# Smaller stated times for VectorE's eigenvector operations, a second weight's sums moved, and fewer operations behind the last broadcast product

## The chip, the cores and the metric

The kernel runs on one core of one Trainium2 chip. The metric is the device time of one execution in microseconds (us), given as the median of several runs. Engines are named as in the profile: PE (TensorE's matmuls), PEld (its weight loads), DVE (VectorE), ACT (ScalarE), POOL (GpSimd) and SP (SyncE, which issues most of the DMAs).

## The reference, cut to what matters

A batch of 128 graphs of 64 nodes with 256 features (8192 rows) goes through four layers, each `x = layernorm(x + layer(x))`. Layer 0 is three graph convolutions. Layer 1 goes through the eigenvectors `U` of a Laplacian of the one 64x64 matrix `adj`. Layer 2 (LSTMs over windows) and layer 3 (attention) follow.

```python
# layer 0: aggregate with adj*S (S is adj here), three weights
weighting = adj * S
h = relu(einsum('nm,bmh->bnh', weighting, x @ W1))
h = relu(einsum('nm,bmh->bnh', weighting, h @ W2))
out = einsum('nm,bmh->bnh', weighting, h @ W3)
# layer 1
deg = sum(A, axis=0) + sum(A, axis=1) - diagonal(A)
L_norm = d_inv_sqrt[:, None] * (diag(deg) - A) * d_inv_sqrt[None, :]
_, U = eigh(L_norm)
h = relu(einsum('mn,bnd->bmd', U.T, features) @ W1 + b1)
out = einsum('nm,bmd->bnd', U, h @ W2 + b2)
```

`eigh` is therefore needed once, on a 64x64 matrix, before layer 1 can begin. It doesn't depend on layer 0.

## The kernel before, in words

**Layer 0 and the eigenvectors run together.** The function `layer0` walks over 16 groups of 512 rows. For a group, `burst` mixes rows with the squared adjacency (64x64 blocks), `weigh` applies the first weight, `seven` computes the second and (except in the last two groups, which use `plain`) the third weight's product by a Strassen scheme of seven block products, and `mix_rows` mixes the result and adds it to the rows. All of these put matmuls on PE; DVE makes the sums of blocks and adds PE's results (`VL`), ACT copies and applies relu. `sums_of_weights` makes four sums of blocks of a weight on DVE, once for the second weight and once for the third.

**The eigenvector pass** is the generator `eigen`. It tridiagonalizes the matrix in 62 steps of 24 DVE instructions, one matmul (`mm(pq, L, AQ)`) and two ACT operations each, bisects for the eigenvalues in six passes, runs a chain of 63 pairs (`t`, named `tw` in the profile, then `D2`, named `D`), and finds the eigenvectors. Nearly all is on DVE, in operations on 64x1 to 128x64 elements. At its end it broadcasts two columns over a matrix with `rows` (the eigenvalues `lam`, then the product `co_[7]`), decides signs (`co_[9]` to `co_[12]`), multiplies (`pu`), and spreads `U` and its transpose into the two 128x128 block matrices `u2` and `ut2`, which layer 1 needs.

**How the two are put in order.** The order of instructions on PE, DVE and ACT is the order in which Python emits them (`manual_schedule`). Python keeps a clock `now`, which each layer-0 matmul advances by a stated time. After each matmul `between()` resumes `eigen` if the time it asked for has come. `eigen` knows its own time by `free[0]`: the class `Timed` passes each DVE operation on and adds a stated time, `least` plus 0.0009 us for each element over 64. `soon()` asks to be resumed 0.45 us before `free`, `full()` at `free`; `until` is the stated time at which a result of PE or ACT is there. So `least` doesn't change what DVE computes: it sets how far apart `eigen`'s instructions are put in the queues, and after which of layer 0's matmuls its own matmuls stand on PE. When layer 0 has been emitted, `while eig:` emits what is left of `eigen`.

```python
self.free[0] = max(self.free[0], self.until[0]) + self.least + 0.0009 * max(0, np.prod(out.shape[1:]) - 64)
```

Before, `least` is 0.25 us at first and for `VL`; 0.285 in the bisection, 0.22 in the chain of pairs, and 0.25 after it.

**After layer 0**, `phase_a.close()` gives back its buffers, the LSTM weights are loaded by SP, and a planner (`Plan`, with its own stated costs) orders layers 1 to 3; all of its instructions carry the helper line L162. Its first matmuls are those of layer 1, `ps<-u,X`. In the profile, DVE operations of `layer0` and `eigen` carry L52, layer 0's matmuls L966 (`burst`: L1031), the eigenvector pass's matmuls L312 (`mm`) and the transposes L323, L644 and L739; ACT's square roots in the steps are L397, its copies behind `burst` L1037.

Of the kernel before, what the change touches and what calls it, by code (L numbers as in the profile page):

```python
# [13 lines left out]
ALU = mybir.AluOpType  # L14
AX = mybir.AxisListType

N = 64
# [24 lines left out]
class Timed:  # L42
# [1 line left out]


    def __init__(self, engine, free, until):
        self.engine, self.free, self.until, self.least = engine, free, until, 0.25

    def __getattr__(self, name):
        def give(out, *args, **kw):  # L50
# [224 lines left out]
def eigen(tc, stack, a, ident, cst, u2, ut2, now, free):  # L275
# [10 lines left out]
    until = [0.0]  # L286
    V, S, PE = Timed(nc.vector, free, until), nc.scalar, nc.tensor
# [5 lines left out]
    def sb(shape, tag):  # L293
        uid[0] += 1
        return wp.tile(shape, F32, tag=tag, name=f"{tag}_{uid[0]}")

    def ps(shape, tag):
        uid[0] += 1
        return pp.tile(shape, F32, tag=tag, name=f"{tag}_{uid[0]}")

    W = 2 * N
    C = {n: cst[:N, i, :] for i, n in enumerate(CONSTS)}
    C["eye"] = ident[:N, :N]

    def soon():
        return max(free[0], until[0]) - 0.45

    def full(turns=0):
        return max(free[0], until[0]) + 0.6 * turns

    def mm(out, lhsT, rhs):
        PE.matmul(out, lhsT, rhs, start=True, stop=True)  # L312
        now[0] += 0.2
        until[0] = now[0] + 0.5
# [46 lines left out]
    eye = C["eye"]  # L361
# [20 lines left out]
    for i in range(N - 2):  # L382
# [9 lines left out]
                               op1=ALU.mult, accum_out=rest)  # L392
# [6 lines left out]
        for update in late[1:]:  # L399
# [11 lines left out]
                               op1=ALU.mult, accum_out=v)  # L411
# [11 lines left out]
                               op1=ALU.mult, accum_out=av)  # L423
# [4 lines left out]
                               op1=ALU.mult, accum_out=c2)  # L428
# [47 lines left out]
    def rows(col, n, tag):  # L476
        b = sb([N, N], "bc")
        V.tensor_scalar(b, C["ones"], col, None, op0=ALU.mult)
        yield full()
        p = ps([N, n, N], tag)  # L480
        mm(p, b, cst[:N, 0:n, :])
        return p

    co = cp.tile([N, 20], F32, name="co")
    co_ = [co[:, j:j + 1] for j in range(20)]
    nrm, s1, s1s, s2e, hs = co_[1:6]
# [11 lines left out]
    t0, t1, t2, big, ae, sg = w_[11:17]  # L498
# [6 lines left out]
    lo, h, top, tgt, at, to = co_[14:20]  # L505
# [51 lines left out]
    idx = cst[:, CONSTS.index("idx"), 1:FAN + 1]  # L557
    Q = cp.tile([W, HALF, FAN], F32, name="Q")
    M = cp.tile([W, FAN, HALF], F32, name="M")
    V.least = 0.285  # L560
    yield soon()
    for _ in range(PASSES):
        V.tensor_scalar(h2, h2, 1.0 / (FAN + 1), None, op0=ALU.mult)
# [5 lines left out]
        for k in range(1, HALF):  # L569
# [10 lines left out]
                               op0=ALU.is_lt, op1=ALU.mult)  # L580
# [18 lines left out]
    V.tensor_scalar(dl, d2, lam2, None, op0=ALU.subtract)  # L599
    D2 = cp.tile([W, N], F32, name="D2")  # L600
    V.tensor_copy(D2[:, N - 1:], dl[:, 0:1])
    V.least = 0.22
    for k in range(1, N):
        c = N - 1 - k
        t = sb([W, 1], "tw")
        V.reciprocal(t, D2[:, c + 1:c + 2])
        V.tensor_scalar(D2[:, c:c + 1], t, es2[:, k:k + 1], dl[:, k:k + 1], op0=ALU.mult, op1=ALU.add)
        yield soon()
    V.least = 0.25
    D = cp.tile([N, 2, N], F32, name="D")  # L610
    for k in range(2):
        V.tensor_scalar(D[:, k, :], D2[k * N:(k + 1) * N, :], 1e15, -1e15, op0=ALU.min, op1=ALU.max)
# [35 lines left out]
    rn = co_[13]  # L648
# [55 lines left out]
    V.tensor_mul(co_[7], co_[7], co_[6])  # L704
    pl = (yield from rows(lam, 1, "pa"))[:, 0, :]
    V.tensor_scalar(t0, pl, lam, 1e-12, op0=ALU.subtract, op1=ALU.add)
    V.reciprocal(t0, t0)
    V.tensor_mul(t0, t0, C["off"])
    V.tensor_copy(t1, pl)
    V.tensor_mul(t1, t1, t1)  # L710
    V.tensor_reduce(co_[8], t1, AX.X, ALU.max)
    V.tensor_scalar(co_[8], co_[8], nrm, (8.0 * 2.0 ** -24) ** 2, op0=ALU.mult, op1=ALU.mult)
    pp_ = (yield from rows(co_[7], 1, "pa"))[:, 0, :]
    rowdot(hs, pp_, t0)
    V.tensor_scalar(hs, hs, -1.0, 1.0, op0=ALU.mult, op1=ALU.add)
    V.tensor_mul(hs, hs, hs)
    V.tensor_mul(hs, hs, co_[8])
    yield soon()
    V.tensor_scalar(co_[9], s1, s1, 2.0, op0=ALU.mult, op1=ALU.mult)
    V.tensor_tensor(co_[9], co_[9], hs, ALU.is_gt)  # L720
    V.tensor_scalar(co_[10], s2e, s2e, 2.0, op0=ALU.mult, op1=ALU.mult)
    V.tensor_tensor(co_[10], co_[10], co_[8], ALU.is_gt)
    yield soon()
    V.tensor_scalar(co_[11], s2e, 0.0, -2.0, op0=ALU.is_gt, op1=ALU.mult)
    V.tensor_scalar(co_[11], co_[11], co_[10], 1.0, op0=ALU.mult, op1=ALU.add)
    V.tensor_scalar(co_[12], s1, 0.0, -2.0, op0=ALU.is_gt, op1=ALU.mult)
    V.tensor_scalar(co_[12], co_[12], 1.0, co_[11], op0=ALU.add, op1=ALU.subtract)
    V.tensor_scalar(co_[12], co_[12], co_[9], co_[11], op0=ALU.mult, op1=ALU.add)
    V.tensor_mul(co_[12], co_[12], rn)


    yield full()
# [1 line left out]
    mm(pu, Z, QT)  # L734
    UT = cp.tile([N, N], F32, name="UT")
    V.tensor_scalar(UT, pu, co_[12], None, op0=ALU.mult)
    yield full()
    pt = ps([N, N], "pa")
    PE.transpose(pt, UT, C["eye"])  # L739
    until[0] = now[0] + 0.7  # L740
    U = cp.tile([N, N], F32, name="U")
    V.tensor_copy(U, pt)
    V.memset(u2, 0.0)
    V.memset(ut2, 0.0)
    yield full()
    for out, lhsT in ((u2, UT), (ut2, U)):
        p2 = ps([2 * N, N], "pa")
        for h in range(2):
            mm(p2[h * N:(h + 1) * N, :], lhsT, C["eye"])
        for h in range(2):  # L750
            V.tensor_copy(out[h * N:(h + 1) * N, h * N:(h + 1) * N], p2[h * N:(h + 1) * N, :])


ROWS = 8192
# [76 lines left out]
def kernel(  # L831
# [26 lines left out]
    V, S, PE = nc.vector, nc.scalar, nc.tensor  # L858
# [5 lines left out]
    def tl(pool, shape, tag, **kw):  # L864
        uid[0] += 1
        return pool.tile(shape, F32, tag=tag, name=f"{tag}_{uid[0]}", **kw)
# [7 lines left out]
    pa = phase_a.enter_context(tc.tile_pool(name="pa", bufs=1))  # L874
# [54 lines left out]
    u2 = keep.tile([P, P], F32, name="u2")  # L929
    ut2 = keep.tile([P, P], F32, name="ut2")  # L930
# [34 lines left out]
    def mm(out, lhsT, rhs, start=True, stop=True, **kw):  # L965
        PE.matmul(out, lhsT, rhs, start=start, stop=stop, **kw)  # L966
        now[0] += 2 * max(0.00084 * rhs.free_size(), 0.112)
        between()
# [8 lines left out]
    def quads(c):  # L977
        for m in (slice(0, N), slice(N, P)):
            for h, hs in enumerate((slice(0, N), slice(N, P))):
# [3 lines left out]
    B11, B12, B21, B22 = (aw2[:, r:r + 2, c:c + 512] for r in (0, 2) for c in (0, 512))  # L983
# [14 lines left out]
    second = ((None, B11, B21, B22, tw[:, 2], B12, tw[:, 1], tw[:, 0]),  # L998
              (None, A11, A12, ss[:, 2], A22, ss[:, 0], ss[:, 1], A21))
    third = ((None, D11, D21, D22, tv[:, 2], tv[:, 3], tv[:, 1], tv[:, 0]),  # L1000
             (None, H11, H12, H12, H22, sh[:, 0], sh[:, 1], H21))
    free = [0.0]
    VL = Timed(V, free, now)
    spare = [lambda: tl(pa, [P, D], "spare")]
    pending = []

    def step(then=None):

        while pending:
            pending.pop(0)()  # L1010
        if then:
            pending.append(then)
        if norms:
            norms.pop(0)()
# [4 lines left out]
    def sums_of_weights(w, b12):  # L1019
        VL.tensor_sub(w[7], w[3], b12)  # L1020
        VL.tensor_sub(w[5], b12, w[1])
        VL.tensor_sub(w[6], w[3], w[5])
        VL.tensor_sub(w[4], w[2], w[6])

# [33 lines left out]
    def seven(n, product, c11, c12, c21, c22, last):  # L1058
# [4 lines left out]
        def add(dst, b):  # L1063
            VL.tensor_add(dst, dst, b)
            if last is relu:
                relu(dst, dst)
# [36 lines left out]
    def weigh(t):  # L1103
        p = bank()
        run(p, [(m1[:, k, t * P:(t + 1) * P], aw1[:, k, :]) for k in range(2)])
        step(lambda: relu(h1[:, t, :], p))

    def mix_rows(g, t):
# [3 lines left out]
        def result():  # L1112
            x2 = rows_of(order[g])[:, t:t + 2, :]
            VL.tensor_add(x2, p, x2)
            norms.extend(scalar_norm(tc, small, x2, half, spare))
# [12 lines left out]
    def layer0():  # L1128
        n = NT // 4
        burst(m1, rows_of(order[0]), 0)  # L1130
        step()
        for t in range(4):
            weigh(t)
        step()
        sums_of_weights(second[0], B12)
        for c in (0, 2):
            burst(m2, h1, c)
        step()
        for g in range(n):
            sums_second()  # L1140
            for j in range(2):
                q = [h2[:, 4 * c + 2 * j:4 * c + 2 * j + 2, r:r + 256] for r in (0, 256) for c in (0, 1)]
                for _ in seven(256, by_second(j), *q, relu):
                    pass
                if j == 0 and g + 1 < n:
                    burst(m1, rows_of(order[g + 1]), 0)
                if j == g == 0:
                    sums_of_weights(third[0], D12)
            q = [s3[:, r:r + 2, c:c + P] for r in (0, 2) for c in (0, P)]
            w3 = seven(P, by_third, *q, S.copy) if g < n - PLAIN else plain()  # L1150
            next(w3)
            next(w3)
            if g < n - PLAIN:
                VL.tensor_add(sh[:, 0], H21, H22)
                VL.tensor_sub(sh[:, 1], sh[:, 0], H11)
            for t in range(4):
                if g + 1 < n:
                    weigh(t)
                if t == 0 and g < n - PLAIN:
                    VL.tensor_sub(H21, H11, H21)  # L1160
                    VL.tensor_sub(H12, H12, sh[:, 1])
            for _ in range(4):
                next(w3)
            if g + 1 < n:
                burst(m2, h1, 0)
            next(w3)
            if g + 1 < n:
                burst(m2, h1, 2)
            for t in (0, 2):
                mix_rows(g, t)  # L1170
        step()

    eig.extend([0.0, eigen(tc, phase_a, adst[:N, :], ident, eig_c, u2, ut2, now, free)])
    with tc.manual_schedule(engines={mybir.EngineType.PE, mybir.EngineType.DVE, mybir.EngineType.Activation}):
        pt = bank()
        PE.transpose(pt[:N, :P], adst, ident)
        for h in range(2):
            hs = slice(h * N, (h + 1) * N)
# [64 lines left out]
    V, S, G, Q = (Noted(plan, e) for e in ("DVE", "ACT", "POOL", "SP"))  # L1243
# [585 lines left out]
```

## Time and profile before

| what | value |
|---|---|
| median of 3 runs | 2280.58 us (2280.14 to 2281.84) |
| the profiled execution, its own time | 2277.23 us |
| its span, first to last instruction | 2275.4 us |
| mean granted TensorE clock | 0.995 |
| PE busy | 2233.0 us (98%), 20612 instructions |
| DVE busy | 1772.5 us (78%), 5868 instructions |
| ACT busy | 1189.5 us (52%), 2892 instructions |
| layer 1's first matmul (L162) | at 834.18 us |

The times of instructions below come from the one profiled execution, counted from the start of its span. Its own time is 1.83 us over its span, and 3.35 us under the median of the three timed runs. A "group" is the stretch of layer 0 from one group of 512 rows to the next, 50.5 us of PE's time in the middle of layer 0. An "x4" in a row counts instructions; a matmul of fp32 data stands there as two, so four matmuls of the program are x8.

### The profile page before, as it was taken

The page shows a single profiled execution, that of the slowest core. Times are in us where ns is not written, and L with a number is a line of the kernel's source. Part 1 is how long each engine was busy: PE and PEld are TensorE (multiplying, and loading weights), DVE is VectorE, ACT ScalarE, POOL GpSimd, SP SyncE. Part 2 cuts the span into 40 slices and gives each one's busy share as a digit, 9 for nine tenths or more (in the row PEclk, how much of TensorE's full clock was granted, in tenths as well). Part 3 has the DMA queues.
Part 4 walks back from the last instruction along what each step waited for, and adds up shares of the span by engine and source line. Part 5 has one row for each costly group of instructions (what it writes and reads, how often), then busy time and mean ns, then how long its engine had stood idle before and what let it go on. Part 6 is the DMA issues. An engine that isn't in the chain of part 4 may idle for free.

```text
span 2275.4 us, 52244 instructions
## 1 busy us (share of the span) xinstructions
PE 2233.0 (98%) x20612; PEld 1990.8 (87%) x20612; DVE 1772.5 (78%) x5868; ACT 1189.5 (52%) x2892; POOL 137.0 (6%) x315
## 2 busy tenths in 40 slices
PE   8999999999999989999999999999999999999997
PEld 6888888887788778999999999999999999999985
DVE  5888777776888879765967977977877887578977
ACT  3444444443434435665655655655656555566554
POOL 0000000000000010000100000000010010000012
PEclk9999999999999999999999999999999999999999
DMA  7000000000000031000111211211221211001331
GB/s 245 11 11 11 11 11 11 11 20 11 11 11 1 1 126 57 11 11 20 66 40 48 78 57 50 87 57 41 87 66 40 78 66 39 31 21 65 117 107 59
DMA packets 80117, 107.93 MB, mean 47 GB/s; under 512 B 23296, under 2 KB 64256, under 8 KB 79872
## 3 DMA queue, kind: packets, MB, share of 16 engines
q1 hardware_dynamic: 79520, 104.32, 14.1%
q8 instruction: 162, 2.65, 0.5%
q14 instruction: 83, 0.68, 0.1%
q10 hardware_dynamic: 352, 0.28, 0.0%
HBM read 57.64 MB, written 45.09 MB: 45 GB/s over the span
## 4 chain that ended last, share of the span: by engine, by line
PE 91%; DVE 6%; issue 1%; ACT 1%; DMA 1%; POOL 0%; SPq 0%; ACTq 0%; DVEq 0%; POOLq 0%
PE ps L162 58%; PE ch L966 14%; PE ps L966 10%; PE b L966 7%; PE ps L1031 2%; PE pa L312 1%; DVE w L162 1%; DVE D L52 1%; DVE tw L52 1%; DVE X L162 1%; DVE gates L162 0%; DVE st L162 0%; DVE v L162 0%; ACT gates L162 0%; DVE h L52 0%
## 5 line engine op out<-in xcount | busy, mean ns | idle before, releaser
L162 PE MATMUL ps<-w,wih 128*128 128x128 f32 (+2 forms) x2944 | 572.0, 298 | 0.3 <-ACT gates L162 0.3
L162 PE MATMUL ps<-w,sums 128*128 128x128 f32 (+2 forms) x3104 | 476.3, 293 | 0.1
L162 PEld LDWEIGHTS ps<-w,wih 128*128 128x128 f32 x2944 | 453.1, 191 | 26.5 <-issue 6.8
L162 PEld LDWEIGHTS ps<-w,sums 128*128 128x128 f32 x3104 | 422.7, 191 | 14.3 <-ACT gates L162 1.9
L162 ACT ACTIVATE gates<-gates,cbi 128x256 f32<-128x256 f32 (+4 forms) x736 | 314.0, 479 | 171.8 <-DVE gates L162 169.9
L162 DVE TENSOR_TENSOR gates<-gates,ps 128x512 f32<-128x512 f32 (+4 forms) x408 | 233.7, 583 | 171.1 <-PE ps L162 158.0
L162 ACT COPY gates<-ps 128x512 f32<-128x512 f32 (+4 forms) x408 | 204.2, 506 | 252.3 <-PE ps L162 245.4
L162 PE MATMUL ps<-hs,whh 128*128 128x128 f32 (+1 forms) x896 | 181.2, 284 | 0.1
L162 PE MATMUL ps<-w,whh 128*128 128x128 f32 (+1 forms) x896 | 181.2, 284 | 0.0
L162 ACT ACTIVATE gates<-ps,cbi 128x128 f32<-128x128 f32 (+2 forms) x368 | 119.5, 384 | 42.9 <-PE ps L162 42.5
L162 PEld LDWEIGHTS ps<-hs,whh 128*128 128x128 f32 x896 | 139.8, 191 | 0.3 <-DVE hs L162 0.3
L162 PEld LDWEIGHTS ps<-w,whh 128*128 128x128 f32 x896 | 139.8, 191 | 0.0
L975 ACT ACTIVATE h<-h 128x512 f32<-128x512 f32 x96 | 60.5, 630 | 150.9 <-DVE h L52 150.9
L966 PE MATMUL ch<-m,tw 128*128 128x256 f32 x512 | 124.7, 381 | 3.1 <-ACT h L1077 1.7
L966 PE MATMUL b<-ss,aw 128*128 128x256 f32 x512 | 121.9, 379 | 0.0
L966 PE MATMUL ps<-aw,m 128*128 128x512 f32 x256 | 116.0, 606 | 1.5 <-DMA aw<-in_a_w_dram 1.5
L966 PEld LDWEIGHTS ch<-m,tw 128*128 128x128 f32 x512 | 94.9, 190 | 18.6 <-DVE h L52 3.4
L966 PEld LDWEIGHTS b<-ss,aw 128*128 128x128 f32 x512 | 96.8, 190 | 12.9
L162 POOL TENSOR_SCALAR rs<-mv 128x2 f32<-128x2 f32 x96 | 23.5, 255 | 1325.1 <-DVE mv L162 1323.7
L966 PEld LDWEIGHTS ps<-aw,m 128*128 128x128 f32 x256 | 48.3, 194 | 55.7 <-issue 51.4
L1037 ACT COPY m<-ps 128x512 f32<-128x512 f32 x96 | 51.2, 587 | 75.5 <-PE ps L1031 75.0
L162 PE MATMUL ps<-hs,sums 128*128 128x128 f32 (+1 forms) x448 | 90.6, 284 | 0.0
(373 smaller groups left out, 4139.2 us busy)
## 6 DMA issues: line engine op xcount, KB each, us to landing
far<-w SPq DMA_DIRECT2D x42, 512.0 KB, 2.9
w<-far SPq DMA_DIRECT2D x168, 128.0 KB, 3.1
X<-rest SPq DMA_DIRECT2D x24, 512.0 KB, 3.3
out_dram<-X SPq DMA_DIRECT2D x64, 128.0 KB, 1.8
rest<-XA SPq DMA_DIRECT2D x12, 512.0 KB, 2.6
rest<-X SPq DMA_DIRECT2D x12, 512.0 KB, 2.8
XA<-in_x_dram SPq DMA_DIRECT2D x22, 256.0 KB, 6.9
aw<-in_a_w_dram SPq DMA_DIRECT2D x3, 1024.0 KB, 10.2
```

The lines of the kernel that those rows point to most:

```text
L52: return getattr(self.engine, name)(out, *args, **kw)
L162: getattr(e, name)(*[real(x) for x in args], **{k: real(v) for k, v in kw.items()})
L312: PE.matmul(out, lhsT, rhs, start=True, stop=True)
L966: PE.matmul(out, lhsT, rhs, start=start, stop=stop, **kw)
L975: S.activation(dst, src, AF.Relu)
L1031: PE.matmul(p[h][m, k, t, :], src[hs, t, f], sqT2[hs, hs], start=True, stop=True)
L1037: S.copy(to[:, h, c:c + 2], p[h])
```

## The change

1. **Stated times.** `least` becomes 0.21 for `eigen` from the start (0.25 before), 0.278 in the bisection (0.285), 0.21 in the chain of pairs (0.22) and after it (0.25). `VL`, layer 0's own stated times, is set back to 0.25.
2. **The second weight's sums** (`sums_of_weights(second[0], B12)`, four DVE additions of 128x1024 elements) are emitted in the first group after the second of four `weigh` calls, no longer after the fourth.
3. **The end of `eigen`.** The second broadcast (`rows(co_[7])`) is emitted right after the first; work that doesn't need its result (`co_[8]`, both halves of `co_[10]` to `co_[12]`, the factor `rn`) is emitted while it is under way; behind the product `rowdot(hs, pp_, t0)` stand four more operations where there were thirteen. `u2` is filled straight from `UT`, ahead of the transposition that gives `U`, and the two memsets move ahead of it.

```diff
-        self.engine, self.free, self.until, self.least = engine, free, until, 0.25
+        self.engine, self.free, self.until, self.least = engine, free, until, 0.21
...
-    V.least = 0.285
+    V.least = 0.278
...
-    V.least = 0.22
+    V.least = 0.21
     for k in range(1, N):
...
-    V.least = 0.25
+    V.least = 0.21
...
     V.tensor_scalar(t0, pl, lam, 1e-12, op0=ALU.subtract, op1=ALU.add)
+    V.tensor_copy(t1, pl)
+    pp_ = (yield from rows(co_[7], 1, "pa"))[:, 0, :]
+    there, until[0] = until[0], 0.0
     V.reciprocal(t0, t0)
     V.tensor_mul(t0, t0, C["off"])
-    V.tensor_copy(t1, pl)
     V.tensor_mul(t1, t1, t1)
     V.tensor_reduce(co_[8], t1, AX.X, ALU.max)
     V.tensor_scalar(co_[8], co_[8], nrm, (8.0 * 2.0 ** -24) ** 2, op0=ALU.mult, op1=ALU.mult)
-    pp_ = (yield from rows(co_[7], 1, "pa"))[:, 0, :]
+    yield soon()
+    V.tensor_scalar(co_[9], s1, s1, 2.0, op0=ALU.mult, op1=ALU.mult)
...
+    V.tensor_mul(co_[12], co_[12], rn)
+    V.tensor_mul(co_[11], co_[11], rn)
+    until[0] = max(until[0], there)
+    yield soon()
     rowdot(hs, pp_, t0)
     V.tensor_scalar(hs, hs, -1.0, 1.0, op0=ALU.mult, op1=ALU.add)
-    V.tensor_mul(hs, hs, hs)
-    V.tensor_mul(hs, hs, co_[8])
...
+    V.tensor_scalar(hs, hs, hs, co_[8], op0=ALU.mult, op1=ALU.mult)
     V.tensor_tensor(co_[9], co_[9], hs, ALU.is_gt)
...
     V.tensor_scalar(co_[12], co_[12], co_[9], co_[11], op0=ALU.mult, op1=ALU.add)
-    V.tensor_mul(co_[12], co_[12], rn)
...
     V.tensor_scalar(UT, pu, co_[12], None, op0=ALU.mult)
+    V.memset(u2, 0.0)
+    V.memset(ut2, 0.0)
     yield full()
+    spread(u2, UT)
     pt = ps([N, N], "pa")
     PE.transpose(pt, UT, C["eye"])
     until[0] = now[0] + 0.7
     U = cp.tile([N, N], F32, name="U")
     V.tensor_copy(U, pt)
-    V.memset(u2, 0.0)
-    V.memset(ut2, 0.0)
     yield full()
-    for out, lhsT in ((u2, UT), (ut2, U)):
-        p2 = ps([2 * N, N], "pa")
...
+    spread(ut2, U)
...
     VL = Timed(V, free, now)
+    VL.least = 0.25
...
         for t in range(4):
             weigh(t)
+            if t == 1:
+                sums_of_weights(second[0], B12)
         step()
-        sums_of_weights(second[0], B12)
```

`spread(out, lhsT)` is the old loop's body: two matmuls with the identity and two DVE copies. In the built programs nothing after layer 1's first matmul differs: PE, DVE, ACT, POOL and SP have the same instructions in the same order from there on.

More of the change, by code (lines that the diff above doesn't have):

```diff
@@ L712, in eigen @@
     V.tensor_scalar(co_[8], co_[8], nrm, (8.0 * 2.0 ** -24) ** 2, op0=ALU.mult, op1=ALU.mult)
-    pp_ = (yield from rows(co_[7], 1, "pa"))[:, 0, :]
+    yield soon()
+    V.tensor_scalar(co_[9], s1, s1, 2.0, op0=ALU.mult, op1=ALU.mult)
+    V.tensor_scalar(co_[10], s2e, s2e, 2.0, op0=ALU.mult, op1=ALU.mult)
+    V.tensor_tensor(co_[10], co_[10], co_[8], ALU.is_gt)
+    V.tensor_scalar(co_[11], s2e, 0.0, -2.0, op0=ALU.is_gt, op1=ALU.mult)
+    V.tensor_scalar(co_[11], co_[11], co_[10], 1.0, op0=ALU.mult, op1=ALU.add)
+    yield soon()
+    V.tensor_scalar(co_[12], s1, 0.0, -2.0, op0=ALU.is_gt, op1=ALU.mult)
+    V.tensor_scalar(co_[12], co_[12], 1.0, co_[11], op0=ALU.add, op1=ALU.subtract)
+    V.tensor_mul(co_[12], co_[12], rn)
+    V.tensor_mul(co_[11], co_[11], rn)
+    until[0] = max(until[0], there)
+    yield soon()
     rowdot(hs, pp_, t0)
     V.tensor_scalar(hs, hs, -1.0, 1.0, op0=ALU.mult, op1=ALU.add)
-    V.tensor_mul(hs, hs, hs)
-    V.tensor_mul(hs, hs, co_[8])
-    yield soon()
-    V.tensor_scalar(co_[9], s1, s1, 2.0, op0=ALU.mult, op1=ALU.mult)
+    V.tensor_scalar(hs, hs, hs, co_[8], op0=ALU.mult, op1=ALU.mult)
     V.tensor_tensor(co_[9], co_[9], hs, ALU.is_gt)
[L721 to L727, printed above, removed]
     V.tensor_scalar(co_[12], co_[12], co_[9], co_[11], op0=ALU.mult, op1=ALU.add)
-    V.tensor_mul(co_[12], co_[12], rn)
     yield full()
@@ L736, in eigen, with spread @@
     V.tensor_scalar(UT, pu, co_[12], None, op0=ALU.mult)
+    V.memset(u2, 0.0)
+    V.memset(ut2, 0.0)
     yield full()
+    def spread(out, lhsT):
+        p2 = ps([2 * N, N], "pa")
+        for h in range(2):
+            mm(p2[h * N:(h + 1) * N, :], lhsT, C["eye"])
+        for h in range(2):
+            V.tensor_copy(out[h * N:(h + 1) * N, h * N:(h + 1) * N], p2[h * N:(h + 1) * N, :])
+    spread(u2, UT)
     pt = ps([N, N], "pa")
@@ L742, in eigen @@
     V.tensor_copy(U, pt)
-    V.memset(u2, 0.0)
-    V.memset(ut2, 0.0)
     yield full()
-    for out, lhsT in ((u2, UT), (ut2, U)):
-        p2 = ps([2 * N, N], "pa")
[L748 to L751, printed above, removed]
+    spread(ut2, U)
 ROWS = 8192
```

## The prediction

> **What bounds the kernel now.** I read the page first: PE is busy for 98% of the span, and the chain that ended last is 91% PE. So time can only be won where PE stands idle or runs at a lower clock, and lost where it is made to wait. PE's timeline up to 900 us shows such places; two are touched here.
>
> The end of the eigenvector pass (PE's timeline; in brackets the idle time ahead of a row and who ended it):
>
> ```profile
> 826.36 1.98 PE L966 MATMUL ps<-s,sqT 128*128 128x512 f32 x4
> 828.18 0.38 PE L1187 MATMUL ps<-adT,ones 128*128 128x128 f32 x2
> 828.75 0.29 PE L312 MATMUL pa<-eig_c,bc 64*64 64x64 f32 x2 [0.19 <-DVE bc L52]
> 829.99 0.33 PE L312 MATMUL pa<-AQ,Z 64*64 64x64 f32 x2 [0.95 <-DVE junk L52]
> 832.72 0.24 PE L739 MATMUL pa<-ident,UT 64*64 64x64 f32 x1 [2.40 <-DVE UT L52]
> 833.27 0.33 PE L312 MATMUL pa<-ident,UT 64*64 64x64 f32 x4 [0.31 <-DVE U L52]
> 834.16 0.37 PE L312 MATMUL pa<-ident,U 64*64 64x64 f32 x2 [0.56 <-DVE u L52]
> ```
>
> Layer 0's last matmul ends at 828.56; layer 1's first starts at 834.18. Between them PE has 1.2 us of work and 4.4 us of idle time: the eigenvector pass ends late, with nothing to cover it.
>
> The start (PE's and DVE's timeline):
>
> ```profile
> 25.64 3.78 PE L966 MATMUL ch<-m,aw 128*128 128x256 f32 x8 [3.57 <-ACT m L1037]
> ...
> 46.50 1.89 PE L966 MATMUL ch<-ss,tw 128*128 128x256 f32 x8
> 48.23 1.03 PE L966 MATMUL b<-ss,aw 128*128 128x256 f32 x4
> ```
> ```profile
> 18.40 0.28 DVE L52 TENSOR_SCALAR AQ<-pa,c 64x64 f32<-64x64 f32 x1 [3.67 <-PE pa L312]
> 18.60 1.21 DVE L52 TENSOR_TENSOR tw<-aw 128x1024 f32<-128x1024 f32 x1
> ```
>
> PE stands for 3.57 us, because ACT's copies wait behind a square root (L397, 24.44), which waits for DVE, which from 18.60 to 23.52 makes the second weight's sums. The eight matmuls behind the gap take 3.78 us; eight such take 1.73 later (46.50 to 48.23, start to start). The granted clock says why (PE busy in column 2, clock after the counts):
>
> ```profile
> 21.54:24.96 3.42, 0.53 (x37) 0.39 (x28) 2.85 (x10) 0.52 (x2) 0.00 (x0) 1.00 1.10 349
> 24.96:28.37 3.41, 2.73 (x7) 2.19 (x8) 1.75 (x3) 1.59 (x4) 0.00 (x0) 0.50 1.10 349
> 28.37:31.78 3.41, 3.41 (x10) 2.69 (x9) 1.38 (x5) 0.59 (x1) 0.00 (x0) 0.50 1.07 338
> ```
>
> From 50 to 550 us PE is never idle for more than 0.15 us. The counterpart is DVE's slack, in DVE's waits from 79.6 to 231 us (three groups):
>
> ```profile
> DVE junk L52 <- PE pa L312: 10.8, 13, 1.4
> DVE XA L52 <- PE ps L966: 3.7, 4, 1.5
> DVE q L52 <- ACT q L397: 2.1, 4, 0.7
> ```
>
> With the smaller rows it is 19.0 us, 6.3 us a group: DVE gets to a point early and waits for a matmul that Python placed late.
>
> **What the skill says.** "TensorE: Matmul & The Clock Gate" (Part 1: The HAM clock gate) has PE fall to half clock after an idle window of about 3.4 us, on a free-running grid. The trace agrees on window and halves: windows with PE busy 15% (above), 17% (830.50) and 33% (2264.08) are followed by clock 0.50, ones with 48% and 53% (2182.16, 847.56) are not. The same page (Part 2) keeps matmuls in program order, and its table makes the other engines' queues strict FIFO; so a matmul put ahead of its operand stops all of PE, as the 2.40 us above. "Vector Engine (DVE) Microarchitecture Reference" (5.2 Measured stream behaviour) gives 1.04 ns a column plus about 75 ns an instruction. 512-column additions agree (0.60 us apart), but dependent one-column operations don't: the chain's pairs stand 0.507 us apart, so I price small ones by the trace.
>
> **The change, part by part.**
>
> *Stated times, tail.* The built orders have the same 78 eigenvector matmuls; before, none of layer 0's stands behind the last, after, 262 PE instructions do, which by the rows' durations is about 79 us. So `u2` is there long before layer 1. Its first matmul still needs DVE: `ps1`'s bank is free after one of the last row additions or `rs_row`, both at DVE's end; 828.56 plus 0.7 gives 829.3, not 834.2: **-4.9**. The half clock from 833.9 to 837.3 loses 3.4/2 = 1.7: it goes, **-1.7**. But ACT must now normalize the last rows (four operations, 829.24 to 831.4 before, in the shadow of the tail) beside layer 1's copies: **+1.0** (0 to 2). Sum -5.6. Behind it the streams are the same, so the shift should carry to the end. The 5 MB of LSTM weights, issued at 826.20 and busy to about 841, are first needed near 867: not late.
>
> *Sums of the second weight.* In the new order they come behind `dm` (14.26) instead of 18.60, so DVE is done at 19.2, but AQ's and LV's memsets now stand behind them, ACT's LV copy behind these, and three relus behind that copy. By durations: relus end 21.3, the bursts 22.7, the step's matmul 23.1, the square root starts 24.0, PE 25.2: **-0.4** (+1 to -1.5). But PE now works between 19 and 23, so the worst window is some 37 to 46% busy: I take it that the clock stays up: **-3.1** (half of 25.64 to 31.78; 0 if not).
>
> *Stated times, steps.* Between two groups' block sums DVE has 163 instructions before and about 192 after: 29 more are 1.2 steps. A group's DVE time without waits is 44.4 us (79.6 on); less 13.0 for layer 0's 19 operations that is 5.2 a step, near 4.8 by 433 us. So 1.2 steps add 6.3 us to a wait of 6.3: DVE is full in the first four groups, later keeps about 2 us (waits 8.3, added 5.9). The stated step, 24 x 0.21 = 5.04, is about true; at 0.25 it was 6.0. Where the slack is gone, a wait left over reaches PE; I take 0.5 us in each of four groups: **+2.0** (0 to +6).
>
> *Chain of pairs and the end.* A pair takes 0.507 and is stated as 0.42 (0.44 before): 63 pairs make DVE 5.5 us late against 4.2. Before, that cost PE 1.33 us at 793 and 0.20 at 798. After, the last busy group holds 39 pairs (19.8), 19 of layer 0's (13.0), 88 others (0.21 each, 18.7): 51.5 against 49.6 of PE, and six exchanges with PE at 0.3: 3.7; less the 1.5 of before: **+2.0** (-1.5 to +5). Bisection fits: a pair stands 0.555 apart, stated 0.556.
>
> *Fewer operations behind the product.* 2.7 us (829.7 to 832.4) shrink to about 1.0, but the end is covered by layer 0 now: **0**; were that cover gone, -1.7. Moved memsets and `spread` likewise 0. No step that moves issues a DMA, and POOL's and SP's orders stay as they were.
>
> **Sum:** -5.6 - 0.4 - 3.1 + 2.0 + 2.0 = -5.1 on the profiled 2277.23, 2272.1. That execution lies 3.35 under the median; the same shift gives **2275.5** for the median. 0.2% is 4.6 us, about what a measurement of this kernel can tell from no change.
>
> **Rivals.**
> 1. *Slower: DVE in lockstep.* With no lead left, each step's `mm` (62) meets a column copy not quite done, and PE pays the hop; 0.31 us as ahead of 833.27. 62 x 0.31 = 19.2 in place of 2.0: 2275.5 + 17.2 = **2292.7**. It turns to slower by 0.2% at 0.19 us a step. For it: DVE's slack is used up early; against it: PE's matmuls are some 4% slower than Python's clock (a group's stated times sum to 48.3, its span is 50.5), which gives DVE about 2 us a group.
> 2. *Cold start.* The window's grid falls on the gap: -5.1 + 3.1, **2278.6**. For it: 37% is near 33%, which fell.
> 3. *The tail is only traded.* Layer 1 then waits for DVE and ACT (DVE is full from 848 to 880): 2 of 5.6 come through, **2279.1**. Against: those stretches start later by the same amount.
> 4. *No move:* refuted by the orders.
>
> **How the numbers follow.** Main case 0.58 (beyond 0.2%: 0.47), cold start 0.16 (0.02), traded tail 0.13 (0), lockstep 0.13 (slower 0.11). Faster 0.49, same 0.39, slower 0.12. Low end: no new stalls (-5.1 - 2.0 - 3.5), 2270. High end: the middle of rivals 1 and 3, 2284; it leaves out about 0.15.
>
> **What would show it.** Right: layer 1's first matmul right behind L1196 (before: L1187), no half clock there; clock 1.00 from 15 us on; DVE's waits for `pa` under 2 us a group to 400 us. Wrong: PE idle `<-DVE LV` in many steps (rival 1), clock 0.50 near 25 us (2), a new gap of PE past 829 us (3).

## The result and the profile after

The changed kernel takes **2308.43 us** (median of 4 runs, 2306.11 to 2309.28), the kernel before 2280.61 us beside it; the ratio is 1.012, 95% interval 1.0102 to 1.0137. The forecast was 2275.5 us: it missed by 33 us, and on the wrong side.

The profiled execution of the changed kernel took 2307.74 us (span 2306.0). Layer 1's first matmul starts at 860.01 us where it started at 834.18, so 25.8 us are lost ahead of it. What follows takes 1445.9 us against 1441.3. The order of instructions there is the same on every engine, and 1441.3 comes from an execution that was 3.4 us under its kernel's median; one experiment below has 1441.3 too, again in an execution 3.4 us under its median, and the others lie between 1442.7 and 1445.7. I don't ascribe this part to the change.

What was foreseen at the end is there. PE's timeline of the kernel after (start, duration, instruction; in brackets the idle time ahead of it and who ended it):

```profile
857.89 1.96 PE L973 MATMUL ps<-s,sqT 128*128 128x512 f32 x4
859.69 0.38 PE L1196 MATMUL ps<-adT,ones 128*128 128x128 f32 x2
860.01 0.33 PE L162 MATMUL ps<-u,X 64*64 64x64 f32 x2
860.84 2.09 PE L162 MATMUL ps<-u,X 64*64 64x64 f32 x126 [0.51 <-DVE rs_row L1197]
```

No eigenvector matmul is left here; one wait of 0.51 us stands where 4.4 us were idle. The loss lies earlier, in a line of the page that I had not thought about. The group of layer 0's Strassen products on the sums `tw`, after (busy time, mean ns; then the idle time of PE ahead of them, and what ended it):

```profile
L973 PE MATMUL ch<-m,tw 128*128 128x256 f32 x512 | 128.1, 389 | 26.1 <-DVE h L52 14.0 <-ACT h L1085 12.0
```

The same group before:

```profile
L966 PE MATMUL ch<-m,tw 128*128 128x256 f32 x512 | 124.7, 381 | 3.1 <-ACT h L1077 1.7 <-DVE h L52 1.2
```

So PE waits for layer 0's own additions on DVE (`h`, L52) and copies on ACT (L1085). And DVE is not full: this is the table of busy time in the stretch of groups 1 to 8 (PE, PEld, DVE, ACT, POOL, then the clock), first of the kernel before, then of the kernel after.

```profile
79.60:483.40 403.80, 403.80 (x3585) 336.36 (x3584) 320.55 (x1500) 181.38 (x480) 17.55 (x48) 1.00 0.03 12
```
```profile
87.20:513.70 426.50, 411.97 (x3599) 335.17 (x3598) 356.72 (x1756) 179.43 (x493) 17.46 (x48) 1.00 0.03 11
```

DVE works 356.7 of 426.5 us, 84%; PE is idle for 14.5 us at full clock. Two engines that both have time to spare wait for each other.

The second place is at the start, on DVE (timeline of the kernel after), and what it does to PE:

```profile
39.12 1.28 DVE L52 TENSOR_TENSOR tv<-aw 128x512 f32<-128x512 f32 x2
44.98 0.16 DVE L1202 TENSOR_TENSOR dbb<-dbb,dbl 128x2 f32<-128x2 f32 x1 [4.58 <-DMA dbb<-in_d_b_dram]
45.05 1.41 DVE L52 TENSOR_TENSOR tv<-aw,tv 128x512 f32<-128x512 f32 x2
```
```profile
25.60 1.99 PE L973 MATMUL ch<-m,aw 128*128 128x256 f32 x8 [2.06 <-ACT m L1045]
...
52.68 2.07 PE L973 MATMUL ch<-m,tw 128*128 128x256 f32 x4 [5.31 <-ACT h L1085]
```

The first row is the start as I predicted it: a shorter gap, and eight matmuls at full clock (1.99 us, 3.78 before). The second is new. `dbb` is a bias of layer 3, added up by a line that stands outside the hand-ordered part. The scheduler placed it in DVE's queue, behind the first sums `tv`. It waits 4.58 us there for its DMA, everything behind it waits too, and PE stands for 5.31 us and then runs four instructions in 2.07 us, where eight took 1.99 (the granted clock is 0.50 from 52.23 to 55.64).

Where the 25.8 us arise, by stage. A mark is DVE's first `ss<-m` of a group; the column "to L162" runs from group 15's mark to layer 1's first matmul, and "idle" is PE's idle time between 50 and 560 us (gaps over 0.15 us that begin there, so without the 5.31 us).

| kernel | group 1 at | groups 1-8 | 9-11 | 12-14 | to L162 | L162 at | idle |
|---|---|---|---|---|---|---|---|
| before | 79.6 | 403.8 | 152.5 | 151.3 | 47.0 | 834.2 | 0.6 |
| after | 87.2 | 426.5 | 147.8 | 158.4 | 40.1 | 860.0 | 15.4 |
| difference | +7.6 | +22.7 | -4.7 | +7.1 | -6.9 | +25.8 | |

The +22.7 and the -4.7 belong together: the 62 steps now end in group 8, where they ended in group 10, so 55 steps lie in groups 1 to 8 instead of 48.

### The profile page after: what moved, and what is told of

Read it like the earlier page. It is cut to its first block, busy times and chain, and to the rows that moved or that the text cites. A ratio compares the mean times of both kernels' runs of the same rounds, so it can differ in the third digit from the quotient of the medians.

```text
span 2306.0 us, 52262 instructions
## 1 busy us (share of the span) xinstructions
PE 2243.8 (97%) x20612; PEld 1990.2 (86%) x20612; DVE 1771.4 (77%) x5868; ACT 1185.0 (51%) x2892; POOL 136.5 (6%) x315
## 4 chain that ended last, share of the span: by engine, by line
PE 87%; DVE 8%; DMA 2%; ACT 1%; issue 1%; SPq 0%; POOL 0%; ACTq 0%; DVEq 0%; POOLq 0%
PE ps L162 59%; PE ch L973 12%; PE ps L973 9%; PE b L973 5%; PE ps L1039 2%; DVE h L52 1%; DVE q L52 1%; PE pa L312 1%; DVE ss L52 1%; DVE D L52 1%; DMA aw<-in_a_w_dram 1%; DVE xr L52 1%; DMA XA<-in_x_dram 1%; DVE junk L52 0%; DVE w L162 0%
## 5 line engine op out<-in xcount | busy, mean ns | idle before, releaser
L162 PE MATMUL ps<-w,wih 128*128 128x128 f32 (+2 forms) x2944 | 572.1, 298 | 0.3 <-ACT gates L162 0.3
L162 PEld LDWEIGHTS ps<-w,wih 128*128 128x128 f32 x2944 | 453.5, 191 | 26.8 <-issue 7.1
L162 PE MATMUL ps<-w,sums 128*128 128x128 f32 (+2 forms) x3104 | 476.0, 293 | 0.0
L162 PEld LDWEIGHTS ps<-w,sums 128*128 128x128 f32 x3104 | 422.7, 191 | 13.8 <-ACT gates L162 1.6
L162 ACT ACTIVATE gates<-gates,cbi 128x256 f32<-128x256 f32 (+4 forms) x736 | 314.2, 480 | 171.1 <-DVE gates L162 169.2
L162 DVE TENSOR_TENSOR gates<-gates,ps 128x512 f32<-128x512 f32 (+4 forms) x408 | 233.9, 584 | 173.9 <-PE ps L162 161.0
L162 ACT COPY gates<-ps 128x512 f32<-128x512 f32 (+4 forms) x408 | 204.2, 506 | 252.7 <-PE ps L162 245.8
L162 PE MATMUL ps<-hs,whh 128*128 128x128 f32 (+1 forms) x896 | 181.4, 284 | 0.1
L162 PE MATMUL ps<-w,whh 128*128 128x128 f32 (+1 forms) x896 | 181.1, 284 | 0.0
L162 ACT ACTIVATE gates<-ps,cbi 128x128 f32<-128x128 f32 (+2 forms) x368 | 119.5, 384 | 43.5 <-PE ps L162 43.1
L162 PEld LDWEIGHTS ps<-hs,whh 128*128 128x128 f32 x896 | 140.0, 192 | 0.3 <-DVE hs L162 0.3
L162 PEld LDWEIGHTS ps<-w,whh 128*128 128x128 f32 x896 | 139.7, 191 | 0.0
L973 PEld LDWEIGHTS ch<-m,tw 128*128 128x128 f32 x512 | 94.0, 192 | 51.2 <-DVE h L52 21.6
L162 POOL TENSOR_SCALAR rs<-mv 128x2 f32<-128x2 f32 x96 | 23.5, 256 | 1329.7 <-DVE mv L162 1328.4
L162 PE MATMUL ps<-hs,sums 128*128 128x128 f32 (+1 forms) x448 | 90.6, 284 | 0.0
L162 ACT ACTIVATE gates<-c 128x256 f32<-128x256 f32 (+1 forms) x176 | 75.5, 433 | 27.3 <-DVE c L162 26.0
```

Source lines behind the costliest of these rows:

```text
L162: getattr(e, name)(*[real(x) for x in args], **{k: real(v) for k, v in kw.items()})
```

## The experiments

My first theory (A in the texts on record) was that the smaller stated times put too much eigenvector work into DVE's queue ahead of layer 0's additions; B was the bias addition; C that one of the other two parts costs it. "before" below is the kernel before, run beside each.

**1. The parts alone.** `old_times` is the changed kernel with 0.25, 0.285, 0.22 and 0.25:

```diff
-        self.engine, self.free, self.until, self.least = engine, free, until, 0.21
+        self.engine, self.free, self.until, self.least = engine, free, until, 0.25
...
-    V.least = 0.278
+    V.least = 0.285
...
-    V.least = 0.21
+    V.least = 0.22
     for k in range(1, N):
...
-    V.least = 0.21
+    V.least = 0.25
```

> The changed kernel with all four stated times as they were (0.25, 0.285, 0.22, 0.25); the sums' new place and the shorter end stay. Theory A (the smaller stated times of the steps put layer 0's additions behind too much eigenvector work in DVE's queue): nearly all of the loss is gone, 2274 to 2281, and PE's idle time behind products of the second kind (ch<-m,tw) falls from 26 us to about 3. Theory B (the bias addition that waits for its DMA on DVE near 45 us, brought forward by the sums' new place): about 5 to 8 us of loss stay if it waits here too, 2281 to 2287. Theory C (the sums' place or the end's new order costs it): 2300 or more.

Measured: 2300.17 us, 1.009 of before (1.0075 to 1.0105). Theory A fails: without any smaller stated time 20 us of loss are still there. The time is one that theory C had named, and C's two parts are told apart below. `only_times` is the kernel before with the four smaller times and no other edit (`VL.least = 0.25` kept):

> The kernel before with the four smaller stated times and nothing else. Theory A: 2300 to 2312, the sum of the loss in the steps and the gain of the covered tail, without the 3 us that the sums' place won. Theory B (bias addition with the sums' place): the wait of 4.6 us isn't there, and the time is 2285 or less. Theory C: 2278 or less.

Measured: 2303.45 us, 1.0105 (1.009 to 1.012), in the range of theory A: the smaller times alone cost as much. `only_steps` has just the first of them:

```diff
-        self.engine, self.free, self.until, self.least = engine, free, until, 0.25
+        self.engine, self.free, self.until, self.least = engine, free, until, 0.21
```

> The kernel before with the smaller stated time in the tridiagonal steps alone (0.25 to 0.21), bisection, chain of pairs and end as before. Theory A with all of it in the steps: 2295 to 2305. Theory A2, in which the chain of pairs and the bisection carry the loss: 2272 to 2278, since the tail is covered by steps that begin 60 us earlier. Theory C: no more than 2281.

Measured: 2296.33 us, 1.0073 (1.0058 to 1.0088). The three smaller times behind the steps therefore cost 7.1 us more. In the two profiles 5.6 of them arise in groups 12 to 14 (154.0 us here, 159.6 in `only_times`); 1.1 arise ahead of group 1, where the two programs are the same, and aren't an effect of these times. `sums_only`, run later, is the kernel before with the sums moved and nothing else:

```diff
         for t in range(4):
             weigh(t)
+            if t == 1:
+                sums_of_weights(second[0], B12)
         step()
-        sums_of_weights(second[0], B12)
```

> The kernel before with the second weight's sums at their new place and nothing else; stated times, holds and the end as before. By the built order its steps stand at 9.0, 17.3, 24.0, 31.2, 42.1 and 50.7 us of group 1, as with the changed kernel's old times. Theory P: this one move costs what the old times kept, 2297 to 2303. If the end's new order had a part in it: 2285 to 2292.

Measured: 2301.28 us, 1.0095 (1.008 to 1.011). The sums alone cost 21.6 us, the times alone 23.3, both and the end's new order together 28. Each alone already does most of the damage, so it isn't work that adds up; it looks like a good state that either edit leaves. `old_times` and `sums_only` differ in the end's new order alone; their times lie 1.1 us apart, which isn't clear of noise.

**2. The bias operations.**

```diff
-    V.tensor_add(dbb, dbb, dbl)
+    nc.gpsimd.tensor_add(dbb, dbb, dbl)
```

and the same for the four beside it.

> The changed kernel with the five small operations on late biases (dbb, cbi, wide c_b0) on POOL instead of DVE; every DVE instruction else in its order. Theory B: the gap of PE of 5.3 us at 47 us goes, and the half clock behind it, 2298 to 2302. If DVE would only wait elsewhere for the same time: 2306 to 2309. Theory A says the rest, some 20 us over the kernel before, stays in either case.

Measured: 2303.17 us, 1.0101 (1.0084 to 1.0118), 5.3 us under the changed kernel. Group 1 begins at 82.4 us instead of 87.2, and groups 1 to 8 take 426.5 us as they did. So B is true for about 5 us, a little less than I expected of it, and for no more.

**3. Where the steps fall.** In the built orders I counted where each step's matmul (`pa<-AQ,LV`) stands in its group, in us of the matmuls placed ahead of it (a group is 52.7 to 52.9 in this count):

```
before       group 1    4.7  14.3  20.1  27.2  38.8  44.8
             group 4-9  0.4  11.0  19.3  25.9  37.9  43.9       (six groups, all the same)
old_times    group 1    9.0  17.3  24.0  31.2  42.1  50.7
             group 6    7.7  16.0  22.7  29.7  40.6  48.4       (creeps down)
only_steps   group 1    9.5  16.9  22.7  28.8  38.8  43.7  51.8
             group 3    7.3  14.3  19.7  25.5  34.0  41.4  48.0
             group 5    9.5  16.9  22.7  28.8  38.8  43.7  51.8 (repeats every four groups)
```

At 0.25 six steps take as long as a group, so the steps stay at one place in it, and in the kernel before that place costs nothing. Moving the sums starts them elsewhere. At 0.21 some seven and a quarter go into a group, so they walk through every place. The groups' lengths follow the places: in `only_steps` groups 1 and 5 take 55.2 and 54.3 us, 2 and 6 take 54.6 and 53.6, 3 and 7 take 51.5 and 51.0, against 50.5 before. This is theory P. Its test adds no instruction, only a wait on Python's clock, to `old_times`:

```diff
     late = []
+    yield now[0] + 6.0
     for i in range(N - 2):
```

> The changed kernel with all four stated times of before, and one line more: the tridiagonal steps are held back by 6 us of Python's clock before the first one. No instruction is added. By the built order the six steps of each group then stand at 0.4, 11.0, 19.3, 25.9, 37.9 and 43.9 us of the group's matmuls, in every group, as in the kernel before from group 4 on; without the hold they stand at 9.0, 17.3, 24.0, 31.2, 42.1, 50.7 and creep down by 0.2 to 0.4 us a group. Theory P (where the steps fall between layer 0's products decides whether its additions come in time): the groups take 50.5 us again instead of 51 to 55, some 14 us less than without the hold: 2282 to 2287 if the bias addition still waits on DVE near 45 us, 2277 to 2281 if it doesn't. Theory A (too much eigenvector work in DVE's queue): the work is the same, so 2297 to 2303.

Measured: 2280.92 us, 1.0002 (0.9994 to 1.0011): one line gives back 19.3 us, with the same DVE work, and the bias addition still waiting 5.05 us. Groups 1 to 8 take 404.1 us (421.8 without the line). The other way round, the kernel before with the bias operations on POOL is held by 12 us or by 14:

```diff
     late = []
+    yield now[0] + 12.0
     for i in range(N - 2):
```

> The kernel before with a hold of 12 us ahead of the first tridiagonal step, and the five bias operations on POOL, so that the hold can't bring them ahead of their DMAs. Its steps stand at 9.0, 17.3, 24.0, 31.2, 42.1, 50.7 in group 1. Theory P: the groups take 52 to 55 us where they took 50.5, 12 to 18 us in all, and the eigenvector pass ends 1 to 4 us later: 2293 to 2302. Theory A: only the later end costs, 2281 to 2285.

```diff
+    yield now[0] + 14.0
```

> The same with a hold of 14 us. Its steps stand at 0.4, 11.0, 19.3, 25.9, 37.9 and 43.9 from group 1 on, one step less in the first group. Theory P: no loss in the groups (50.5 us), but the eigenvector pass ends one step later, 5 to 9 us of idle PE at its end: 2285 to 2290, so less than with a hold of 12 us although it is held longer. If the hold itself costs (theory A): more than with 12 us.

Measured: 2289.95 us (1.0043, 1.0028 to 1.0058) with 12, and 2276.92 us (0.9987, 0.998 to 0.9993) with 14. The longer hold is 13 us faster; groups 1 to 8 take 420.1 and 404.2 us. Both came out lower than I wrote, since group 1 begins at 74.4 and 71.4 (before: 79.6), which I had not counted. The bias operations don't explain that: in the kernel before they don't wait on DVE at all (`dbb` at 45.48, no idle time ahead of it), though no run has the POOL edit alone on that kernel. The hold takes the steps' work away from the start: the gap of 3.57 us ahead of 25.64 and the half clock behind it are gone, and the same eight matmuls start at 22.51 and 21.35. The later end of the pass is there as expected: 53.0 us to L162 with 14, before 47.0.

**4. How a place costs time.** PE in `old_times`, then DVE:

```profile
143.83 1.99 PE L973 MATMUL ch<-m,tw 128*128 128x256 f32 x8 [0.16 <-ACT h L1085]
145.66 0.59 PE L973 MATMUL b<-ss,aw 128*128 128x256 f32 x2
146.09 0.38 PE L312 MATMUL pa<-AQ,LV 128*128 128x128 f32 x2
146.31 1.46 PE L973 MATMUL b<-ss,aw 128*128 128x256 f32 x6
148.67 1.99 PE L973 MATMUL ch<-m,tw 128*128 128x256 f32 x8 [0.90 <-DVE h L52]
```
```profile
146.51 0.26 DVE L52 SCALAR_TENSOR_TENSOR junk<-pa,q,xr 64x51 f32<-64x51 f32 x1 [1.98 <-PE pa L312]
...
147.64 0.26 DVE L52 SCALAR_TENSOR_TENSOR xr<-xr,q,xr 64x50 f32<-64x50 f32 x1
147.93 0.69 DVE L52 TENSOR_TENSOR h<-h,ch 128x512 f32<-128x512 f32 x1
```

Product 7 of the Strassen scheme ends near 145.8. DVE must add it (`h<-h,ch`) before product 4 may write `ch` again, and product 3 (`b<-ss,aw`, 1.73 us) is there to hide that. But the step's matmul stands inside product 3. DVE, idle since 144.5, waits 1.98 us for it, then does the operations behind it, and only then the addition: product 4 waits 0.90 us. In `hold6` the step's matmul stands inside product 4:

```profile
141.46 1.89 PE L974 MATMUL b<-ss,aw 128*128 128x256 f32 x8
143.19 0.59 PE L974 MATMUL ch<-m,tw 128*128 128x256 f32 x2
143.62 0.38 PE L312 MATMUL pa<-AQ,LV 128*128 128x128 f32 x2
143.84 1.46 PE L974 MATMUL ch<-m,tw 128*128 128x256 f32 x6
```
```profile
140.98 0.19 DVE L52 COPY LV<-u 64x64 f32<-64x64 f32 x1
141.73 0.69 DVE L52 TENSOR_TENSOR h<-h,ch 128x512 f32<-128x512 f32 x1 [0.57 <-PE ch L974]
```

Here the addition waits for its own product and for nothing else. The code says why the order can turn out either way: `step` puts an addition off until the next product has been placed,

```python
        product(ch, 7, False)
        step(lambda: add(c22, ch))      # kept in pending
        yield
        product(b5, 3, False)           # between() after each matmul: eigen may emit here
        step(lambda: add(c12, b5))      # only now the addition of c22 is emitted
```

so whatever `eigen` emits during product 3 stands ahead of it in DVE's queue. The step's matmul need not stand in product 3 itself. Here, in `old_times` again, it stands in product 7, and the operations that wait for it still come ahead of the addition:

```profile
251.65 0.38 PE L312 MATMUL pa<-AQ,LV 128*128 128x128 f32 x2
...
252.31 1.89 PE L973 MATMUL b<-ss,aw 128*128 128x256 f32 x8
255.30 1.99 PE L973 MATMUL ch<-m,tw 128*128 128x256 f32 x8 [1.10 <-DVE h L52]
```
```profile
252.08 0.25 DVE L52 SCALAR_TENSOR_TENSOR junk<-pa,q,xr 64x39 f32<-64x39 f32 x1 [1.25 <-PE pa L312]
...
254.56 0.69 DVE L52 TENSOR_TENSOR h<-h,ch 128x512 f32<-128x512 f32 x1
```

How far this reaches can be counted. Groups 1 to 8 have 16 rounds of the second weight's seven products. In `old_times` product 4 waits in 12 of them, 10.4 us in all: in nine rounds with a step's matmul in product 7 (8.2 us) and in three with one in product 3 (2.2 us). Over the groups 1 to 8 of all fourteen profiles (some have the same order there):

| the round has a step's matmul | rounds | product 4 waits in | us in all |
|---|---|---|---|
| in product 7 | 63 | 55 | 44.3 |
| else in product 3 | 32 | 26 | 21.1 |
| else in product 5 | 15 | 8 | 2.6 |
| in none of these | 114 | 0 | 0 |

In these groups the kernel before, `hold6` and `before_hold14` have no step's matmul in product 7 or 3; the kernel before has two in product 5, without a wait. Not all waits are of this kind: in `old_times` PE also stands for 3.0 us in seven waits of product 7 for ACT's copy of `ch` (L1085).

**5. Keeping them out by rule.** In the changed kernel with the bias operations on POOL, `eigen` is not resumed during products 3 and 5:

```diff
-        while eig and eig[0] <= now[0]:
+        while eig and eig[0] <= now[0] and not quiet[0]:
...
+        quiet[0] = True
         product(b5, 3, False)
+        quiet[0] = False
```

The same two lines stand around product 5.

> The changed kernel with the bias operations on POOL, and with the eigenvector work held while Python places the products 3 and 5 of each seven (b<-ss,aw), so that no step's matmul, and no DVE operation that waits for one, comes between the pending addition h<-h,ch and the product that needs it. Theory P in its exact form (a step's matmul in product 3 or 5 makes DVE wait ahead of the addition): PE's idle time in the steps falls from 15.6 us to 3 or less, wherever the steps stand; the steps' pitch grows from 7.25 to 8.12 us, so the pass ends later and some of the tail is open again: 2280 to 2290 instead of 2303. If DVE were just overfull with steps of 0.21 (theory A): the gaps stay, 2298 to 2305.

Measured: 2285.95 us, 1.0028 (1.0017 to 1.004), 17.2 us under the same kernel without the rule. The idle time in the steps falls from 15.6 to 6.3 us, not to 3. In groups 1 to 8 the waits of product 4 are nearly gone (9.8 us, now 0.8); those of product 7 for ACT's copy are not (4.6 us, now 5.0). This second path is seen in this kernel's DVE and ACT timelines:

```profile
150.48 0.26 DVE L52 SCALAR_TENSOR_TENSOR AQ<-xr,u,AQ 64x49 f32<-64x49 f32 x1
150.78 0.69 DVE L52 TENSOR_TENSOR h<-h,ps 128x512 f32<-128x512 f32 x1
```
```profile
151.50 0.63 ACT L984 ACTIVATE h<-h 128x512 f32<-128x512 f32 x1 [3.00 <-DVE h L52]
152.03 0.57 ACT L1087 COPY h<-ch 128x512 f32<-128x512 f32 x1
```

The addition of product 2 comes late behind the eigenvector work that DVE still has, ACT waits 3.00 us with the relu of that sum, and the copy of `ch`, which PE needs, stands behind the relu. At 152.66 PE has been idle for 1.02 us. No run took this path away by itself, so that it is the steps' place which opens it is read from this timeline and from its absence in `hold6`, not tested apart. `quiet_chain` also states 0.25 in the chain of pairs:

```diff
-    V.least = 0.21
+    V.least = 0.25
     for k in range(1, N):
```

> The same with 0.25 stated for an operation of the chain of pairs instead of 0.21, which is what a pair takes on the chip (0.507 us). If the stalls of the chain's groups (5.6 us in the changed kernel) come from Python's clock running ahead of DVE there: they fall to 1 or less, while the pass ends up to 5 us later; 2272 to 2284, between 1 and 5 less than with 0.21. If not: the same as with 0.21 or more.

Measured: 2286.78 us, 1.0029 (1.0019 to 1.0039), no different from 0.21. The rule alone had brought the idle time of 560 to 800 us from 5.6 to 1.3 us; the true time took away the 1.3, the end of the pass took 0.9 more, and nothing that can be measured is left.

**6. A version that beats both.** The changed kernel with 0.25 in the steps, its own smaller times behind them, the hold of 6 us and the bias operations on POOL:

```diff
-        self.engine, self.free, self.until, self.least = engine, free, until, 0.21
+        self.engine, self.free, self.until, self.least = engine, free, until, 0.25
...
+    yield now[0] + 6.0
...
-    V.tensor_add(dbb, dbb, dbl)
+    nc.gpsimd.tensor_add(dbb, dbb, dbl)
```

> The changed kernel with 0.25 in the tridiagonal steps, its own smaller times in bisection, chain and end (0.278, 0.21, 0.21), the hold of 6 us, and the five bias operations on POOL. Theory P: groups of 50.5 us, no wait of the bias addition, the 3.5 us of the sums' new place kept, and a shorter end of the pass: 2270 to 2276, faster than both kernels. If the chain of pairs stalls as in the changed kernel (5.6 us): 2276 to 2281. Theory A: 2290 or more.

Measured: **2275.39 us, 0.9979 (0.997 to 0.9987)**. L162 starts at 829.8, 4.4 us earlier than in the kernel before, and all of that is won ahead of group 1 (74.6 us, before 79.6): the later stages take 404.2, 152.3, 151.9 and 46.8 us, within 0.6 us of before. The end, which I had expected shorter, is not. Adding the rule from group 11 on, where the chain of pairs lies:

```diff
         for g in range(n):
+            late[0] = g >= 11
...
+        quiet[0] = late[0]
         product(b5, 3, False)
+        quiet[0] = False
```

> The version with the hold of 6 us, 0.25 in the steps, the changed kernel's smaller times behind them and the bias operations on POOL, and with the eigenvector work held during products 3 and 5 from group 11 on, where bisection, chain and end lie. If the chain's stalls there (4.4 us of PE's idle time from 560 to 800 us) are of the same kind as in the steps, they fall to about 1, and the pass ends later by at most as much: 2270 to 2275, up to 4 us under the version without it. If the work held only comes out behind layer 0: 2275 to 2278, no gain.

Measured: 2278.92 us, 0.9995 (0.9987 to 1.0003). The chain's idle time fell from 4.4 to 1.3 us as expected, but the pass ended later, and the idle time behind 800 us rose from 1.9 to 8.8: more than was won.

## Why the prediction was wrong, point by point

- **Tail (-5.6): right up to layer 1's first matmul, not behind it.** The stretch to L162 fell from 47.0 to 40.1 us, L162 stands behind L1196, and the clock there was 1.00. But the half clock that I booked as gone (-1.7) only moved: it lay at 833.92 to 837.33 and lies at 874.84 to 878.25 now, behind a wait of PE of 2.48 us (at 873.62) that the kernel before doesn't have. This is the sign that I had named for rival 3; what PE waits for there the profile doesn't show.
- **Second weight's sums (-0.4 - 3.1): the local reading was partly right, the step as a whole failed.** In place of -3.5 the stage ahead of group 1 has +7.6 us. The gap fell from 3.57 to 2.06 us, though PE restarted at 25.60 and not at 25.2. The full clock behind it was luck (see the last section). What I left out is that the move also shifts everything behind it: the starting place of the 62 steps, and one operation that isn't in the hand-made order. I had written that no moved step issues a DMA and looked no further; an operation that *waits* for one had come forward. The move alone cost 21.6 us.
- **Stated times, steps (+2.0): this step failed.** I compared DVE's work in a group with its waits, got "full in the first four groups", and charged what was over. Measured in groups 1 to 8: +22.7 us (+18.0 with groups 9 to 11), with DVE busy 84% of the time. The load was about right (1.2 more steps a group were predicted; 7 or 8 came where there were 6, until the steps ran out in group 8) and beside the point. What counted was whether a step's result is waited for between an addition's operand and the product that needs the addition. Before, PE never waited in these groups because no step's matmul stood in a product 7 or 3, and I took that for slack.
- **Chain of pairs and the end (+2.0): too small.** Right in kind, too small in size: `only_times` less `only_steps` is 7.1 us, 5.6 of it in groups 12 to 14. PE's waits for layer 0's additions and copies begin among the pairs (0.92, 0.20 and 2.07 us at 719 to 739 in the kernel after, where the pairs lie from 699 on), not only at the end where I put them. These stalls weren't taken apart as those of the steps were.
- **Fewer operations behind the product (0):** not contradicted. Its cover, layer 0, was there. With the old times, where a part of the end is uncovered, it makes 1.1 us (`old_times` against `sums_only`), not clear of noise; I had written 1.7 for an uncovered end.
- **The rivals.** Lockstep came nearest in size (2292.7), with a real exchange between DVE and PE, but at another place: PE never waited for `LV` in a step. It named the matmul whose operand comes from DVE; the waiting went the other way, DVE for that matmul, with layer 0's addition behind it. The sign that I named for the right case was a poor one: I read DVE's waits for `pa` as slack, but between 50 and 560 us they are 36.7 us in `hold6` and 71.0 us in `old_times`, with the same work. In these runs such a wait cost PE time in most rounds where it could lie ahead of product 7's addition (81 of 95, products 7 and 3), and none at product 4 in the 114 rounds where no step's matmul stood near. The high end was also added up wrongly: the middle of rivals 1 and 3 (2292.7 and 2279.1) is 2285.9 and not 2284, which changes nothing here.

## What to carry to other kernels

When two streams share queues that keep their order, slack in busy time says little (here DVE was busy for 84% and PE waited all the same). Ask, for each result that the critical engine needs back, what stands ahead of it in the other engine's queue, and whether that waits for the critical engine itself. If a kernel shows no such wait anywhere, check in the built order whether the streams are in step with each other (six steps to a group here); then any edit of the period, or of anything ahead of the first step, can change the result by more than its own work, and a plain delay is an experiment that tells it apart at once. And look at what the scheduler adds to a hand-made order: a two-column addition on a late DMA stopped three engines.

## What the runs showed of the hardware

- **A stall costs more than the idle time that the profile shows.** In groups 1 to 8 of `old_times` PE is idle for 13.5 us, but the stretch is 17.7 us longer than in `hold6` with as many matmuls: over 19 stalls that is 0.22 us more for each. `before_hold12` against `before_hold14` gives the same (15.9 us, 11.8 of them idle, 18 stalls: 0.23). The ends of matmuls are modelled in the profile, so this may be work or idle time; no run here shows where in a stall it lies.
- **The same gap can be warm or cold.** PE stands for 2.06 us near 25 us in `sums_only` and in the changed kernel. In the first the clock fell to half, in the second it didn't (PE busy, and the clock behind the counts; first `sums_only`, then after):

```profile
24.00:26.00 2.00, 0.92 (x3) 0.83 1.12 350
26.00:28.00 2.00, 2.00 (x6) 0.50 1.02 329
```
```profile
24.00:26.00 2.00, 0.40 (x2) 1.00 1.09 356
26.00:28.00 2.00, 2.00 (x11) 1.00 1.10 350
```

"TensorE: Matmul & The Clock Gate" of the Trainium skill (Part 1: The HAM clock gate) puts the windows on a free-running grid, and the runs agree. In `sums_only` the half clock runs from 25.32 to 28.73, so the window of 3.41 us ahead of it begins at 21.91 and holds the whole gap: PE is busy for 1.35 us of it (40%). In the changed kernel (half clock from 52.23, so an edge falls at 24.92) the gap lies across two windows, busy for 2.01 and 2.74 us. Of the six profiles with this gap, `sums_only` and `bias_on_pool` (1.35 us as well) were followed by the half clock; the changed kernel, `old_times`, `quiet_pool` and `quiet_chain` were not, and the least busy of their windows around the gap has 1.81 us (53%, `quiet_pool`). PE's order there is the same in `bias_on_pool` and the changed kernel. So the 3.1 us that I booked as won come in some profiled executions and not in others, and should have been booked as a chance.
